# Two quarters of the last pair turned by TensorE, their input loaded early, and the last two products laced

## The chip, the cores and the metric

The kernel runs on one core of one Trainium2 chip. The metric is the device time of one execution in microseconds (us), the median over several runs; smaller is better. A profiled execution, taken by the hardware profiler, gives the trace from which the rows below come.

## The reference

One transformer-like block on `x` of 2 x 2048 x 512 in float32, with a condition vector per batch that gives six rows of shifts, scales and gates:

```python
emb = jnp.dot(jax.nn.silu(t), ada_w) + ada_b
shift_msa, scale_msa, gate_msa, shift_mlp, scale_mlp, gate_mlp = jnp.split(emb, 6, axis=-1)
norm = _ln(x) * (1.0 + scale_msa[:, None]) + shift_msa[:, None]
h = jax.nn.gelu(jnp.dot(norm, ssm_w1) + ssm_b1, approximate=False)
ssm_out = jnp.dot(h, ssm_w2) + ssm_b2
x = x + gate_msa[:, None] * ssm_out
norm2 = _ln(x) * (1.0 + scale_mlp[:, None]) + shift_mlp[:, None]
hf = jax.nn.gelu(jnp.dot(norm2, ff_w1) + ff_b1, approximate=True)
ff_out = jnp.dot(hf, ff_w2) + ff_b2
x = x + gate_mlp[:, None] * ff_out
```

`ff_w1` is 512 x 1024 and `ff_w2` 1024 x 512. The last two lines are the part that the change touches.

## The kernel before

The 4096 rows are cut into eight blocks of 512. The first half of the block (norm1, ssm1, ssm2, norm2) runs block by block; its result x1 goes to DRAM (`x1_d`). The feed-forward then takes the blocks in four pairs (`s` = 0 to 3): `up(s)` makes the hidden layer, `down(s)` the output. All products are made by Strassen's scheme in two levels: an outer product of a pair is cut into seven (P1 to P7), each of these again into seven *leaves* (P1 to P7), and a leaf is two matmuls of 128 x 128 by 256, four rows `128x256` in the trace.

**Order of TensorE's work.** `ff()` writes it out by hand in *slots*: the product number n starts at slot 7n, and its leaves stand two slots apart, in the order P1, P5, P6, P2, P7, P3, P4. So the second half of one product's leaves alternates with the first half of the next one's: the two are *laced*. `down` takes its products in the order P1, P2, P3, P6, P5, P7, P4. In the kernel before, the very last product (P4 of `down(3)`) starts six slots later (`starts[-1] += 6`) and is not laced: P7's leaves end first.

**Order of the other engines' work.** The class `Plan` collects every operation with its costs; `order()` gives each a latest time (`late`) by going back from the due times of TensorE's work, and `simulate()` plays the engines with these costs and picks, on each engine, the operation that is ready with the earliest latest time. Additions out of SBUF may go to VectorE or GpSimd (`"vg"`), whichever the simulation gives them to. The order that comes out is fixed for the chip. The outputs at the very end have no successor; for those that are named in `plan.closing` the due time is the end of TensorE's planned work plus 6000 ns.

**A quarter's way out.** The result of a pair stands transposed (features by rows) in `summed`, four quarters `r` = 0 to 3 of 128 x 2 x 512: r0 is finished by P2, r3 by P5, r2 by P7 and r1 by P4. r0 and r3 belong to the pair's first and second block in the first half of the columns and come from `quarter_out(s, 0, ...)`; r1 and r2 are the first and second block in the other half. To be added to x1 and stored, a quarter must be turned back. `quarter_out` (line 1065) does this in steps: two activations (bias and gate) by ScalarE, two transpositions of 32 x 32 blocks by VectorE into `bands` (`far` in the trace), four stores to DRAM (`back<-far`), one load back (`rows<-back`), the load of x1 into `rest` (`far<-x` or `near<-x`), two additions and two stores of the output. In the last pair the stores alternate between the queues of SP and ACT. For r1 and r2 of the last pair the gate is folded into the accumulation (`scaled_add`, line 1049), with the bias put in ahead by ScalarE.

In the kernel before, r1 of the last pair alone leaves by another way, `last_out`: as each of its four pieces (`quad`: half e of the columns, half h of the rows) is finished by a leaf, TensorE turns it in two transpositions of 128 x 128 (`turn_by_pe`, line 306) into a PSUM bank, VectorE adds it to x1, which was loaded into `near`, and the piece is stored, by SP's queue for e = 0 and by ACT's for e = 1. The turning of a piece stands one leaf behind the leaf that finished it.

The names of the trace: `rows` is `summed`, `hidden` the hidden layer of the pair, `near` and `far` hold operands, sums, `bands` and `rest`, and `back` is the DRAM copy. L258 is an addition (`tt`), L276 and L285 ScalarE's work, L296 a matmul, L306 a transposition by TensorE, L318 any DMA, L1049 `scaled_add`, L1073 a transposition by VectorE.

Of the kernel before, what the change touches and what calls it, by code (L numbers as in the profile page):

```python
# [20 lines left out]
class Plan:  # L21
# [67 lines left out]
    def order(self):  # L89
        ops = self.ops  # L90
        for op in ops:
            if op.engs == "p":
                op.deps = {d for d in op.deps if ops[d].engs != "p"}
            for d in op.deps:
                ops[d].succ.append(op.n)
        t, due = 0.0, {}
        for op in ops:
            if op.engs == "p":
                due[op.n] = t
                t += op.cost["p"]  # L100
        due.update((n, t + 6000.0) for n in self.closing)
        for _ in range(2):
            for op in reversed(ops):
                late = due.get(op.n, 1e9)
                for s in op.succ:
                    late = min(late, ops[s].late - (1 + op.care) * (self.HOP + min(op.lat.values()) + op.size / self.RATE))
                op.late = late - op.sooner
            self.simulate()
            wait = ops[self.anchor].start - due[self.anchor]
            due = {n: t + wait for n, t in due.items()}  # L110
        return sorted(ops, key=lambda op: (op.start, op.n))
# [89 lines left out]
def kernel(  # L201
# [21 lines left out]
    C = 4  # L223
# [836 lines left out]
    def rest_in(s, d, blk, x):  # L1060
        half = slice(d * D // 2, (d + 1) * D // 2)
        dma(x, x1_d[2 * s + blk][:, :, half])
        return x, out_blk[2 * s + blk][:, :, half]

    def quarter_out(s, d, blk, r, scaled=False):
        done = summed[:, r]
        n = quarters[0] % 2
        for e in range(0 if scaled else 2):
            act(done[:, e], done[:, e], AF.Identity, *columns(s, d, e, blk))
        band = cut(bands[n], "p (a c e r) -> p e c a r", a=M, c=C, e=2)  # L1070
        for e in range(2):
            o, a = band[:, e], cut(done[:, e], "p (c a q) -> p c a q", c=C, a=M)
            plan.add("v", lambda E, o=o, a=a: E.transpose(o, a), [o], [a], {"v": 636}, {"v": 705})  # L1073
        closing = s + 1 == NBLK // 2
        queue = lambda f: "sa"[f % 2] if closing else "s"
        far_t = back_d[s][d][blk]
        for f in range(M):
            dma(far_t[:, f].rearrange("(a q) r -> q a r", a=M), cut(bands[n][f * G : (f + 1) * G], "p (a r) -> p a r", a=M), queue(f))
        flat = done.rearrange("p e t -> p (e t)")
        dma(flat, far_t.rearrange("p f r -> p (f r)"))  # L1080
        x, to = rest_in(s, d, blk, rest[n])
        for h in range(2):
            c = slice(2 * h, 2 * h + 2)
            o = cut(x[:, c], "p c (e f r) -> p (c e) f r", e=2, f=M)
            a = cut(flat, "p (f c e r) -> p c e f r", f=M, c=C, e=2)[:, c].rearrange("p c e f r -> p (c e) f r")
            tt("v" if closing else "vg", o, a, o, ALU.add)
            if closing:
                dma(to[:, c], x[:, c], queue(h))
                plan.closing.append(plan.ops[-1].n)
        if not closing:  # L1090
            dma(to, x)
        quarters[0] += 1

    def down(s):
# [22 lines left out]
        def leaf(n, f):  # L1117
            p = DOWN[n]
            bank = chain_banks(14 * s + 7 + n)
            t = bank[BANK[f]][:, :HT]  # L1120
            for k in range(2):
                mm(t, fw2_leaves[p][f][:, k, :], inner[n][f][:, k, :], f in ("P1", "P5") and k == 0, f in ("P2", "P3", "P4") and k == 1)
            if f == "P1":
                copy(bank["x"][:, :HT], t)
                return
            quad = QUAD[f]
            e, h = int(quad[0]) - 1, int(quad[1]) - 1
            new = f not in ("P7", "P3")
            part = summed[:, :, e, h * HT : (h + 1) * HT]
            r0, r1, r2, r3 = [part[:, r] for r in range(4)]  # L1130

            def add(o, a):
                tt("v", o, t, a, ALU.add)

            if p in ("P1", "P3"):
                o = r1 if p == "P1" else r3
                if new:
                    copy(o, t)
                else:
                    add(o, o)  # L1140
            elif p == "P2":
                add(r0, r1 if new else r0)
                if f == "P4":
                    quarter_out(s, 0, 0, 0)
            elif p == "P6":
                add(r1, r1)
            elif p == "P5":
                add(r2, r1 if new else r2)
                if f in ("P2", "P7", "P3", "P4"):
                    tt("vg", r3, r3, r2, ALU.add)  # L1150
                    if last:
                        act(part[:, 1:3], part[:, 1:3], AF.Identity, *columns(s, 1, e, 0))
                if f == "P4":
                    quarter_out(s, 0, 1, 3)
            elif p == "P7":
                both, wide = part[:, 1:3], t.unsqueeze(1).to_broadcast([P, 2, HT])
                if last:
                    scaled_add(both, wide, columns(s, 1, e, 0)[1])
                else:
                    tt("v", both, wide, both, ALU.add)  # L1160
                if f == "P4":
                    quarter_out(s, 1, 1, 2, last)
            elif not last:
                add(r1, r1)
                if f == "P4":
                    quarter_out(s, 1, 0, 1)
            else:
                scaled_add(r1, t, columns(s, 1, e, 0)[1])
                last_out(s, f, quad)

        return sums, last_sum, prepare, leaf

    tail = {}

    def last_out(s, f, quad):
        if not tail:
            tail["x"], tail["out"] = rest_in(s, 1, 0, cut(kb(near_r, 0, 4), "p (c d) -> p c d", c=C))

        def turned_back(quad):
            e, h = int(quad[0]) - 1, int(quad[1]) - 1  # L1180
            bank = cut(banks[(2, 0)[h]], "p (c e d) -> p c e d", c=2, e=2)
            for c in range(2):
                col = slice((2 * h + c) * P, (2 * h + c + 1) * P)
                turn_by_pe(bank[:, c, e], summed[:, 1, e, col], ident, c == 0 and h not in tail, c == 1)
            tail[h] = True
            c, d = slice(2 * h, 2 * h + 2), slice(e * P, (e + 1) * P)
            x = tail["x"][:, c, d]
            tt("v", x, bank[:, :, e], x, ALU.add)
            dma(tail["out"][:, c, d], x, "sa"[e])

        tail.setdefault("due", [])
        for q in tail["due"]:
            turned_back(q)
        tail["due"] = []
        if f in ("P7", "P2", "P3", "P4"):
            tail["due"].append(quad)
        if f == "P4":
            turned_back(quad)

    def ff():  # L1200
        work, hooks = [], {}

        def at_slot(n, fn):
            hooks.setdefault(n, []).append(fn)

        for s in range(NBLK // 2):
            first_at = 14 * s
            got = {}

            def begin(s=s, got=got):  # L1210
                got["up"] = up(s, tokens(s))

            at_slot(7 * first_at, begin)
            for n in range(7):
                work.append((f"ff1 {s}", lambda n=n, got=got: got["up"][0](n), lambda f, n=n, got=got: got["up"][1](n, f)))
            sums, last_sum, prepare, leaf = down(s)
            at_slot(7 * (first_at + 7) + 7, sums)
            at_slot(7 * (first_at + 7 + 4) + 3, last_sum)
            for n in range(7):
                work.append((f"ff2 {s}", lambda n=n, fn=prepare: fn(n), lambda f, n=n, fn=leaf: fn(n, f)))  # L1220
        total = len(work)
        starts = [7 * n for n in range(total)]
        starts[-1] += 6
        for at in range(starts[-1] + 13):
            for fn in hooks.get(at, ()):
                fn()
            for n in range(max(0, at // 7 - 2), min(total, at // 7 + 1)):
                stage, prepare, leaf = work[n]
                plan.stage = stage
                if at == starts[n]:  # L1230
                    prepare()
                j, odd = divmod(at - starts[n], 2)
                if not odd and 0 <= j < 7:
                    leaf(CARRIED[j])

    def small_loads():
# [204 lines left out]
```

## Time and profile before

| | |
|---|---|
| median of 3 runs | 570.07 us (569.95 to 570.16) |
| the profiled execution's own time | 569.9 us |
| its span, first to last instruction | 568.1 us |
| mean granted clock of TensorE | 0.992 |
| busy: TensorE, VectorE, ScalarE, GpSimd | 553.2, 481.9, 281.6, 391.5 us |
| moved by DMA | 124.73 MB, mean 220 GB/s |

The span is shorter than the execution's time, since the latter has the start and the end around it. Busy times are sums over the whole span, and say little of its end, where the engines fall idle one after another; there the rows of the timeline say when each step began and how long it took.

### The profile page before, as it was taken

What the parts mean: (1) busy time and instruction counts of PE and PEld (TensorE: products, weight loads), DVE (VectorE), ACT (ScalarE), POOL (GpSimd) and SP (SyncE); (2) the same over time, 40 slices, a digit from 0 to 9 for tenths busy, and PEclk for the clock granted to TensorE, in tenths of its full rate; (3) what the DMA queues carried; (4) which work ended last, traced back from release to release, by engine and by line L of the source; (5) the groups of instructions that cost most, each with busy time, mean ns of one, the idle gap of its engine ahead of it and who ended that gap; (6) DMA issues with size and microseconds to landing.
All of it is one profiled execution on the core that took longest, in us unless ns stands there. A gap on an engine that the chain in (4) does not pass through costs nothing. (4 is left out here: it accounts for less than half of the span.)

```text
span 568.1 us, 8720 instructions
## 1 busy us (share of the span) xinstructions
PE 553.2 (97%) x2801; PEld 480.6 (85%) x2801; DVE 481.9 (85%) x841; ACT 281.6 (50%) x521; POOL 391.5 (69%) x476
## 2 busy tenths in 40 slices
PE   8999999999999999999999999999999999999982
PEld 4888889888898988888878888888888888888871
DVE  5696888987878588999999986799987999988993
ACT  3464867574978844665214347224447124353230
POOL 2887747979936399984756776775867777756750
PEclk9999999999999999999999999999999999999996
DMA  8953899988399969993203998404998405963238
GB/s 313 399 217 87 240 355 292 340 260 275 96 285 326 321 245 270 329 299 114 74 2 98 302 336 310 149 1 130 310 342 277 136 0 157 335 205 111 75 101 269
DMA packets 66209, 124.73 MB, mean 220 GB/s; under 512 B 5700, under 2 KB 33268, under 8 KB 64628
## 3 DMA queue, kind: packets, MB, share of 16 engines
q1 hardware_dynamic: 63856, 122.32, 65.3%
q10 hardware_dynamic: 2308, 1.86, 1.2%
q8 instruction: 22, 0.36, 0.3%
q14 instruction: 23, 0.19, 0.1%
HBM read 78.41 MB, written 44.70 MB: 217 GB/s over the span
## 5 line engine op out<-in xcount | busy, mean ns | idle before, releaser
L296 PE MATMUL bank<-turned,ring 128*128 128x256 f32 x896 | 210.2, 380 | 0.2 <-DVE turned L660 0.2
L296 PEld LDWEIGHTS bank<-turned,ring 128*128 128x128 f32 x896 | 167.9, 190 | 23.2 <-DVE turned L660 0.4
L258 DVE TENSOR_TENSOR hidden<-bank,hidden 128x512 f32<-128x512 f32 (+1 forms) x170 | 123.1, 753 | 23.2 <-PE bank L296 19.8
L296 PE MATMUL bank<-near,hidden 128*128 128x256 f32 (+1 forms) x470 | 95.1, 350 | 0.0
L296 PEld LDWEIGHTS bank<-near,hidden 128*128 128x128 f32 x470 | 82.2, 190 | 9.4 <-POOL near L258 0.3
L258 POOL TENSOR_TENSOR turned<-turned 128x512 f32<-128x512 f32 (+1 forms) x65 | 73.6, 1146 | 22.1 <-DVE turned L258 10.2
L296 PE MATMUL bank<-far,fw 128*128 128x256 f32 (+1 forms) x354 | 86.1, 375 | 0.2
L296 PE MATMUL bank<-ring 128*128 128x256 f32 x336 | 82.7, 380 | 0.1
L258 DVE TENSOR_TENSOR rows<-bank,rows 128x256 f32<-128x256 f32 (+1 forms) x142 | 65.9, 477 | 15.4 <-PE bank L296 12.6
L285 ACT COPY bank<-bank 128x512 f32<-128x512 f32 (+2 forms) x84 | 37.7, 449 | 75.2 <-PE bank L296 68.9
L296 PEld LDWEIGHTS bank<-far,fw 128*128 128x128 f32 x354 | 66.5, 190 | 10.0 <-issue 0.5
L296 PEld LDWEIGHTS bank<-ring 128*128 128x128 f32 x336 | 63.5, 190 | 9.8 <-issue 0.5
L276 ACT ACTIVATE hidden<-hidden,cols 128x512 f32<-128x512 f32 (+1 forms) x66 | 44.4, 709 | 42.1 <-DVE hidden L258 42.0
L258 POOL TENSOR_TENSOR hidden<-hidden 128x128 f32<-128x128 f32 (+2 forms) x45 | 45.7, 1025 | 26.7 <-DVE hidden L258 13.2
L296 PE MATMUL bank<-near,fw 128*128 128x256 f32 (+1 forms) x246 | 60.9, 377 | 0.4 <-DVE rows L1049 0.4
L296 PE MATMUL bank<-hidden,fw 128*128 128x256 f32 (+1 forms) x216 | 53.2, 376 | 1.1 <-DVE rows L1049 1.1
L296 PEld LDWEIGHTS bank<-near,fw 128*128 128x128 f32 x246 | 46.3, 190 | 6.9 <-issue 0.8
L276 ACT ACTIVATE turned<-turned,mod,mod 128x512 f32<-128x512 f32 x56 | 42.3, 806 | 9.3 <-DMA turned<-turned 8.9
L296 PEld LDWEIGHTS bank<-hidden,fw 128*128 128x128 f32 x216 | 40.3, 190 | 7.3 <-DVE rows L1049 1.5
L258 POOL TENSOR_TENSOR fw<-fw 128x256 f32<-128x256 f32 (+1 forms) x38 | 35.6, 945 | 12.0 <-DMA fw_parts<-fw 4.4
L258 POOL TENSOR_TENSOR ring<-turned,ring 128x256 f32<-128x256 f32 x41 | 29.8, 738 | 16.8 <-PE bank L296 9.2
L276 ACT ACTIVATE rows<-rows,gb,mod 128x512 f32<-128x512 f32 x32 | 25.5, 812 | 27.0 <-DVE rows L258 18.9
(124 smaller groups left out, 740.5 us busy)
## 6 DMA issues: line engine op xcount, KB each, us to landing
ring<-fw_parts SPq DMA_DIRECT2D x28, 512.0 KB, 4.3
turned<-far SPq DMA_DIRECT2D x52, 256.0 KB, 4.6
ring<-fw_parts SPq DMA_DIRECT2D x28, 384.0 KB, 5.5
turned<-turned SPq DMA_DIRECT2D x32, 256.0 KB, 4.9
rows<-back SPq DMA_DIRECT2D x15, 512.0 KB, 5.7
back<-far SPq DMA_DIRECT2D x54, 128.0 KB, 3.1
fw_parts<-fw SPq DMA_DIRECT2D x21, 256.0 KB, 4.6
fw<-in_L_cond_ada_w_dram SPq DMA_DIRECT2D x5, 1024.0 KB
```

What stands on the lines that cost most here:

```text
L258: lambda E: E.tensor_tensor(o, a, b, f),
L276: lambda E: E.activation(o, a, func, bias=bias, scale=scale),
L285: plan.add("a", lambda E: E.copy(o, a), [o], [a], {"a": cost}, {"a": cost + 60})
L296: lambda E: E.matmul(o, lhsT, rhs, start=start, stop=stop, skip_group_check=True, **kw),
```

## The change

- r2 of the last pair leaves the way r1 does: `last_out` becomes `turned_by_pe(blk, r, ...)`, which serves both. r1 (`blk` 0) is turned into banks 3 and 4, r2 (`blk` 1) into banks 2 and 0. r0 and r3 still go by `quarter_out`.
- The turning of a piece stands two leaves behind the leaf that finished it, counted over P7 and P4 together (their leaves other than P1); what is left after the last leaf is turned then.
- x1 for r1 and r2 is loaded into `hidden`, into the room of an operand of P1 (before: `near` for r1, `far` for r2).
- P4 starts at slot 7n like every other product and is laced with P7. Its operand sums are prepared six slots earlier with it.
- The outputs of r1 and r2 are named in `plan.closing`, and the due time of the closing outputs is the end of TensorE's work plus 3000 ns.

```diff
-        due.update((n, t + 6000.0) for n in self.closing)
+        due.update((n, t + 3000.0) for n in self.closing)
...
-    def quarter_out(s, d, blk, r, scaled=False):
+    def quarter_out(s, d, blk, r):
         done = summed[:, r]
         n = quarters[0] % 2
-        for e in range(0 if scaled else 2):
+        for e in range(2):
             act(done[:, e], done[:, e], AF.Identity, *columns(s, d, e, blk))
...
-                if f == "P4":
-                    quarter_out(s, 1, 1, 2, last)
+                if last:
+                    turned_by_pe(1, 2, f, quad)
+                elif f == "P4":
+                    quarter_out(s, 1, 1, 2)
...
                 scaled_add(r1, t, columns(s, 1, e, 0)[1])
-                last_out(s, f, quad)
+                turned_by_pe(0, 1, f, quad)
...
-    tail = {}
-
-    def last_out(s, f, quad):
-        if not tail:
-            tail["x"], tail["out"] = rest_in(s, 1, 0, cut(kb(near_r, 0, 4), "p (c d) -> p c d", c=C))
-
-        def turned_back(quad):
+    TURNED_AT = ((3, 4), (2, 0))
+    tail, waiting, leaves_read = [{}, {}], [], [0]
+
+    def turned_by_pe(blk, r, f, quad):
+        got = tail[blk]
+        if not got:
+            got["x"], got["out"] = rest_in(NBLK // 2 - 1, 1, blk, cut(kb(hidden_r, 8 * blk, 4), "p (c d) -> p c d", c=C))
+
+        def turned_back():
             e, h = int(quad[0]) - 1, int(quad[1]) - 1
-            bank = cut(banks[(2, 0)[h]], "p (c e d) -> p c e d", c=2, e=2)
+            bank = cut(banks[TURNED_AT[blk][h]], "p (c e d) -> p c e d", c=2, e=2)
             for c in range(2):
                 col = slice((2 * h + c) * P, (2 * h + c + 1) * P)
-                turn_by_pe(bank[:, c, e], summed[:, 1, e, col], ident, c == 0 and h not in tail, c == 1)
-            tail[h] = True
+                turn_by_pe(bank[:, c, e], summed[:, r, e, col], ident, c == 0 and h not in got, c == 1)
+            got[h] = True
             c, d = slice(2 * h, 2 * h + 2), slice(e * P, (e + 1) * P)
-            x = tail["x"][:, c, d]
+            x = got["x"][:, c, d]
             tt("v", x, bank[:, :, e], x, ALU.add)
-            dma(tail["out"][:, c, d], x, "sa"[e])
-
-        tail.setdefault("due", [])
-        for q in tail["due"]:
-            turned_back(q)
-        tail["due"] = []
+            dma(got["out"][:, c, d], x, "sa"[e])
+            plan.closing.append(plan.ops[-1].n)
+
+        n = leaves_read[0] = leaves_read[0] + 1
         if f in ("P7", "P2", "P3", "P4"):
-            tail["due"].append(quad)
-        if f == "P4":
-            turned_back(quad)
+            waiting.append((n, turned_back))
+        done = blk == 0 and f == "P4"
+        while waiting and (done or waiting[0][0] + 2 <= n):
+            waiting.pop(0)[1]()
...
-        starts = [7 * n for n in range(total)]
-        starts[-1] += 6
-        for at in range(starts[-1] + 13):
+        for at in range(7 * (total - 1) + 13):
...
-            for n in range(max(0, at // 7 - 2), min(total, at // 7 + 1)):
+            for n in range(max(0, at // 7 - 1), min(total, at // 7 + 1)):
                 stage, prepare, leaf = work[n]
                 plan.stage = stage
-                if at == starts[n]:
+                if at == 7 * n:
                     prepare()
-                j, odd = divmod(at - starts[n], 2)
-                if not odd and 0 <= j < 7:
+                j, odd = divmod(at - 7 * n, 2)
+                if not odd and j < 7:
                     leaf(CARRIED[j])
```

## The prediction

> **What bounds the kernel now.** I read the page first: it says which engine carries the span as a whole.
>
> ```profile
> span 568.1 us, 8720 instructions
> PE 553.2 (97%) x2801; PEld 480.6 (85%) x2801; DVE 481.9 (85%) x841; ACT 281.6 (50%) x521; POOL 391.5 (69%) x476
> ```
>
> TensorE is busy for 97% of the span, so only the stretches in which it is not can give time back. The view by windows shows where they are (columns: PE, PEld, DVE, ACT and POOL busy, clock, DMA share, GB/s).
>
> ```profile
> 520.00:530.00 10.00, 10.00 (x48) 8.79 (x47) 9.29 (x12) 3.64 (x8) 6.80 (x6) 1.00 0.00 0
> 545.00:550.00 5.00, 3.92 (x18) 3.10 (x18) 4.90 (x9) 3.13 (x5) 5.00 (x5) 1.00 0.00 0
> 550.00:553.00 3.00, 2.71 (x13) 2.05 (x11) 3.00 (x7) 0.36 (x1) 0.27 (x1) 1.00 0.84 203
> 553.00:557.00 4.00, 3.53 (x19) 2.75 (x19) 2.96 (x9) 0.00 (x0) 0.00 (x0) 1.00 1.04 275
> 557.00:568.00 11.00, 0.43 (x2) 0.20 (x2) 3.28 (x6) 0.00 (x0) 0.00 (x0) 0.62 0.81 274
> ```
>
> Three things are to be seen. Up to 545 us TensorE has no gap (the row of 520 to 530 stands for the ones before). From 545 to 553 VectorE is full (7.90 of 8 us) and TensorE is short of 1.4 us: VectorE sets the pace. After 557 both are done and 11 us pass with the DMA engines at 0.81. The change touches only the last two stretches, so I next took the end of the chain of waits (start, us, what), and the transfers of the last quarters by the timeline of SP and ACT.
>
> ```profile
> 557.47 0.43 DVE near L258
> 557.93 5.46 DMA out_dram<-near
> 563.38 0.68 DVE far L258
> ...
> 529.58 0.80 SPq L318 DMA_DIRECT2D back<-far  x2
> 533.36 0.34 SPq L318 DMA_DIRECT2D rows<-back  x1
> 549.57 0.78 SPq L318 DMA_DIRECT2D back<-far  x2
> 552.66 1.45 SPq L318 DMA_DIRECT2D back<-far  x2
> 554.29 0.76 SPq L318 DMA_DIRECT2D rows<-back  x1
> 555.36 0.82 SPq L318 DMA_DIRECT2D far<-x  x1
> 557.37 0.34 SPq L318 DMA_DIRECT2D rows<-back  x1
> 560.88 1.45 SPq L318 DMA_DIRECT2D out_dram<-near  x3
> 564.70 0.38 ACTq L318 DMA_DIRECT2D out_dram<-far  x1
> ```
>
> The chain names a DMA to out_dram as what released the add at 563.38, but an add can't wait for an output of another tile. What it reads is rows, and the rows<-back load issued at 557.37 is r2's: so that load is the true releaser, 6.0 us after its issue. VectorE's rows show both DRAM trips.
>
> ```profile
> 547.37 1.56 DVE L1049 SCALAR_TENSOR_TENSOR rows<-bank,mod,rows 128x512 f32<-128x512 f32 x2
> 548.84 0.70 DVE L1073 STREAM_TRANSPOSE far<-rows 128x512 f32<-128x512 f32 x1
> 550.10 1.32 DVE L258 TENSOR_TENSOR far<-rows,far 128x512 f32<-128x512 f32 x2
> 551.35 1.29 DVE L1073 STREAM_TRANSPOSE far<-rows 128x512 f32<-128x512 f32 x2
> 557.47 0.42 DVE L258 TENSOR_TENSOR near<-bank,near 128x256 f32<-128x256 f32 x1 [0.20 <-PE bank L306]
> 560.16 1.29 DVE L258 TENSOR_TENSOR near<-rows,near 128x512 f32<-128x512 f32 x2 [2.27 <-DMA rows<-back]
> 563.38 1.29 DVE L258 TENSOR_TENSOR far<-rows,far 128x512 f32<-128x512 f32 x2 [1.92 <-DMA out_dram<-near]
> ```
>
> r3 (product P5): second transposition at 548.84, stores from 549.57, load at 554.29, back at 560.16. r2 (product P7): transpositions at 551.35, stores from 552.66, load at 557.37, back at 563.38. From there the two adds, the output issued at 564.70 and its landing take 568.1 - 563.38 = 4.7 us. r1 (product P4), which TensorE turns already, has its last add at 557.47 and ends well before. So the end is set by r2's trip, and 3.2 us before it stands r3's.
>
> **The change part by part.** *r2 leaves the DRAM path.* Gone are two transpositions (1.29 us of VectorE), four stores and one load of 0.5 MB each way, one x1 load in the crowded stretch (555.36) and the two late adds. With r2 gone r3 is late next. If r3's trip stayed as it is, the end would be 560.16 + 4.7 = 564.9, a gain of 3.2 us.
>
> *What r2 costs instead.* Eight transpositions by TensorE and four adds out of PSUM. Their prices stand in the trace for r1:
>
> ```profile
> 544.03 1.03 PE L296 MATMUL bank<-hidden,fw 128*128 128x256 f32 x4
> 546.14 1.99 PE L296 MATMUL bank<-hidden,fw 128*128 128x256 f32 x8 [1.08 <-DVE rows L1049]
> 553.15 1.10 PE L296 MATMUL bank<-near,fw 128*128 128x256 f32 x4 [0.43 <-DVE rows L1049]
> 554.09 0.38 PE L306 MATMUL bank<-far,rows 128*128 128x128 f32 x2
> 554.30 1.03 PE L296 MATMUL bank<-near,fw 128*128 128x256 f32 x4
> 555.17 0.38 PE L306 MATMUL bank<-far,rows 128*128 128x128 f32 x2
> 555.39 1.03 PE L296 MATMUL bank<-far,fw 128*128 128x256 f32 x4
> 556.25 0.42 PE L306 MATMUL bank<-far,rows 128*128 128x128 f32 x2
> ```
>
> A pair of transpositions delays the next matmul by 554.30 - 554.09 = 0.21 us, so r2's four pairs cost TensorE 0.84 us; a leaf takes 0.86 us (555.39 to 556.25). The four adds are 0.42 each, 1.7 us of VectorE, 0.4 more than the transpositions they replace. All of it lies ahead of r1's last add, none of it ahead of r3's load except one or two adds.
>
> *P7 and P4 laced.* After P7's fourth leaf at 544.03 ten leaves are left: 10 x 0.86 = 8.6 us, with r2's 0.84 and one pair of r1's 0.21, which puts the end of the last leaf at 544.03 + 0.86 + 9.7 = 554.6 if nothing stalls, against 556.25 now. VectorE will not allow all of that: it is full from 545 to 553, and its work up to P4's last add only grows by the 0.4 while an add of r1 (0.42) falls behind it. So the end of the products comes earlier by at most what VectorE idles there now, about 1.1 us (553 to 557: 4 - 2.96). I take 0.7: r1's last add ends at 557.2 and its output is out, by the 3.4 us that the output at 564.70 needed, at 560.6, or, by the 5.5 of the chain's row, at 562.7. Either is ahead of r3. If the cover fails, r1 may grow by 1 us before it matters.
>
> *r3's trip gets quieter.* It took 549.57 to 560.16, 10.6 us. The same trip of r0 ran with the DMA engines to itself: stores at 529.58, load at 533.36, last bytes in the slice before 537.0:
>
> ```profile
> 536.50:537.00 0.50, 0.50 (x4) 0.45 (x3) 0.50 (x1) 0.00 (x0) 0.50 (x1) 1.00 0.06 25
> ```
>
> that is 7.4 us. Between these lies the after: during r3's trip r2's 0.5 MB store and the 0.5 MB x1 load fall away and r2's 0.5 MB of output comes in their place, 0.5 MB less, which at 275 GB/s (553 to 557) is 1.9 us. I take 10.6 - 1.9 = 8.7 us. The Trainium skill, DMA: Bandwidth & Descriptors, section "Issuing engines are not separate DMA queues", says that transfers issued from SP and from ACT run on the same 16 engines and interleave; by that rule r2's outputs on ACT's queue hold up r3's trip on SP's, and if they did not, the trip would be the quiet 7.4 and the end 1.3 us sooner. The trace agrees with the rule: a DMA share of 1.04 from 553 to 557, while both queues were at work. The two x1 loads cost nothing: their room is free once P1 is through, and the DMA engines are idle (0.00) from 520 to 530; were they to come after 550 instead, they would add 1.9 us each.
>
> *r3's start.* P4's sums are prepared six steps earlier, so some may fall to VectorE, ahead of r3's transpositions. The nearest rows are P7's sums, which are laced already: VectorE did three of the four, the planner's choice.
>
> ```profile
> 536.33 1.22 DVE L258 TENSOR_TENSOR hidden<-hidden 128x512 f32<-128x512 f32 x1
> 538.67 1.93 DVE L258 TENSOR_TENSOR far<-hidden,far 128x512 f32<-128x512 f32 x1
> 544.61 1.27 POOL L258 TENSOR_TENSOR far<-near 128x512 f32<-128x512 f32 x1 [1.58 <-DVE rows L258]
> L258 DVE TENSOR_TENSOR rows<-rows x3: 410/424/2016, 541.3 to 544.0; 128x256 f32<-128x256 f32 x3
> ```
>
> Now GpSimd does P4's (the row at 544.61 is the first), is free for them from there, and VectorE is the fuller one, so I expect half a sum or so on VectorE, 0.7 us. The bounds: a gain of 0.8 (the closings' due time is 3 us nearer, so the second transposition may pass the 0.78 us scaled add ahead of it) to a loss of 1.9 (one sum at its dearest). The Trainium skill, SBUF — State Buffer, section "Who interferes with whom", speaks against this part: a VectorE instruction with two SBUF inputs is blocked whole while GpSimd reads SBUF. The trace agrees: r3's own sums, rows<-rows, take 410 ns and once 2016. By the rule one of r3's sums could wait out a GpSimd sum of 1.27 us, which is within these bounds.
>
> **The sum.** r3's stores 549.57 + 0.7 = 550.3; back at + 8.7 = 559.0; end at + 4.7 = 563.7, a gain of 4.4 us. The profiled execution took 569.9 us for a span of 568.1, and the median of the runs is 570.07, so 2.0 lies around the span: 565.7 us. Its own range: at best 549.57 - 0.8 + 7.4 + 4.7 = 560.9, 562.9 us; at worst 549.57 + 1.9 + 10.6 + 4.7 = 566.8, 568.8 us. That bytes alone do not bind: from 549.57 on there are r3's store, load and output and the outputs of r0, r1 and r2, 6 x 0.5 MB, at 275 GB/s 11.4 us, which ends at 561.
>
> **The rivals.** *A: r3's load is stuck on SP's queue.* SP issues in the written order, and r1's and r2's outputs now have due times too. An output of r1 on SP waits for TensorE and VectorE; if the planner puts r1's last SP output ahead of r3's load, the load goes at 556.6 to 557.4 instead of 554. Back after 3.6 us (r0's, 533.36 to 537.0) to 6.0 us (r2's), the end is 564.9 to 568.1: 566.9 to 570.1 us. For it: the planner counts a store trip longer than it took (549.57 to 554.29). Against: the load is due ahead of the outputs by its own trip and the adds behind it, so it is taken as soon as the planner holds it to be ready. Chance 0.15.
>
> *B, the slower side: P4's four sums go to VectorE.* Place: VectorE between 543 and 553, where it has 0.1 us to spare. Price: four times 1.2 to 1.9 us, 4.9 to 7.7 us on every add behind them. r1's last add would end at 557.9 + 4.9 to 7.7, and with 3.4 to 5.5 us for its output the span is 566.2 to 571.1; sums of 1.6 us and the output that the chain shows give 557.9 + 6.4 + 5.5 = 569.8, 571.8 us. It is slower from 5.8 us of sums on (557.9 + 5.8 + 5.5 = 569.2, 1.1 above the span now). For: VectorE took three of P7's four. Against: GpSimd is busy only 0.27 us from 550 to 553 and nothing else is planned for it. Chance 0.10.
>
> *C: the trip does not shorten.* r2's outputs and r0's, planned earlier, fill the engines as r2's trip did, and r3's stores come 1.9 us later on top: the upper end of the forecast, 568.8, up to 570. Chance 0.05.
>
> **How the numbers follow.** Forecast 0.70, A 0.15, B 0.10, C 0.05. The predicted time is the forecast's, 565.7. About 0.2% is what a measurement here can tell from no change, 1.1 us: faster means below 568.9. The forecast lies below it, and two thirds of A, one fifth of B, half of C: 0.70 + 0.10 + 0.02 + 0.02 = 0.84, of which I take 0.02 off for the forecast's upper edge: 0.82. Same takes the rest of A and C and that edge, 0.08; slower is most of B and what I can't see, 0.10. The range goes from the forecast's lower end, 562.9, to 569.2, which takes in its upper end and most of A and leaves out B: about 0.15.
>
> **What would show it.** Right: two rows<-back loads after 520 us instead of three; no transposition after r3's; r3's load before 555 and back before 560; the last adds of the span on the near tile, the last output 3 to 4 us before the end; two x1 loads into hidden before 540. TensorE's last instruction at about 556.7. Wrong: r3's load after 556 (A), P4's sums far<-near among VectorE's rows after 543 (B), a trip of more than 10 us from stores to adds (C), or a gap of TensorE before 540, which would mean that the order changed upstream.

## The result, and the profile after

The change takes 565.65 us (median of 4 runs, 565.55 to 565.75) against 570.12 us of the kernel before in the same comparison: a ratio of 0.9921, with a 95% interval of 0.9904 to 0.9938, 4.5 us less. The profiled execution took 565.75 us with a span of 564.0.

The windows of the kernel after, at the end of its span (columns as before: PE, PEld, DVE, ACT and POOL busy, clock, DMA share, GB/s):

```profile
545.00:550.00 5.00, 4.86 (x25) 3.95 (x24) 4.90 (x9) 2.89 (x5) 2.55 (x2) 1.00 0.00 0
550.00:553.00 3.00, 3.00 (x16) 2.37 (x16) 3.00 (x7) 0.00 (x0) 0.00 (x0) 1.00 0.70 165
553.00:557.00 4.00, 3.03 (x19) 2.42 (x17) 3.80 (x11) 0.00 (x0) 0.00 (x0) 1.00 0.84 192
557.00:564.00 7.00, 0.17 (x2) 0.00 (x0) 2.04 (x4) 0.00 (x0) 0.00 (x0) 0.80 0.82 270
```

TensorE's gap of 1.4 us between 545 and 553 is nearly gone (7.86 of 8 us), VectorE is as full as it was, now up to 557, and the stretch after 557 has shrunk from 11 us to 7. The timeline of the kernel after, SP and ACT (DMA issues) and then VectorE and TensorE, shows what stands in it:

```profile
549.99 0.78 SPq L318 DMA_DIRECT2D back<-far  x2
551.68 0.40 SPq L318 DMA_DIRECT2D out_dram<-hidden  x1
553.72 0.40 SPq L318 DMA_DIRECT2D out_dram<-far  x1
554.35 0.34 SPq L318 DMA_DIRECT2D rows<-back  x1
560.15 0.38 ACTq L318 DMA_DIRECT2D out_dram<-near  x1
...
540.87 1.21 DVE L258 TENSOR_TENSOR near<-hidden,near 128x1024 f32<-128x1024 f32 x1
543.73 1.22 DVE L258 TENSOR_TENSOR far<-near,far 128x512 f32<-128x512 f32 x1
548.67 1.29 DVE L1073 STREAM_TRANSPOSE far<-rows 128x512 f32<-128x512 f32 x2
556.99 0.76 DVE L258 TENSOR_TENSOR hidden<-bank,hidden 128x256 f32<-128x256 f32 x2 [0.20 <-PE bank L306]
558.83 1.29 DVE L258 TENSOR_TENSOR near<-rows,near 128x512 f32<-128x512 f32 x2 [1.08 <-DMA rows<-back]
...
555.17 0.38 PE L306 MATMUL bank<-far,rows 128*128 128x128 f32 x2
556.52 0.66 PE L306 MATMUL bank<-far,rows 128*128 128x128 f32 x4 [0.97 <-DVE hidden L258]
```

One load from DRAM is left here, r3's. r1 and r2 are added into `hidden` and the last of these adds ends at 557.75. VectorE then has nothing to do until r3 is back at 558.83. The end of the chain of waits says it too:

```profile
553.09 0.60 DVE far L258
554.35 4.38 DMA rows<-back
558.83 0.69 DVE near L258
559.52 0.60 DVEq L1437
```

The chain doesn't reach the load by way of r3's stores. It comes from r0's first addition (553.09), whose output stands ahead of the load on SP's queue (553.72).

| step | forecast | measured |
|---|---|---|
| r3's stores | 550.3 | 549.99 |
| r3's load | 554 | 554.35 |
| r3 back, adds begin | 559.0 | 558.83 |
| from there to the end | 4.7 | 5.2 |
| span | 563.7 | 564.0 |
| r1's last add ends | 557.2 | 557.75 |

### The profile page after: what moved, and what is told of

The parts are those of the page before. It is cut to its first block, busy times and chain, and to the rows that moved or that the text cites. A ratio compares the mean times of both kernels' runs of the same rounds, so it can differ in the third digit from the quotient of the medians.

```text
span 564.0 us, 8729 instructions
## 1 busy us (share of the span) xinstructions
PE 552.8 (98%) x2809; PEld 481.2 (85%) x2809; DVE 481.4 (85%) x842; ACT 281.7 (50%) x521; POOL 388.5 (69%) x475
## 4 chain that ended last, share of the span: by engine, by line
PE 87%; DVE 7%; DMA 3%; ACT 1%; issue 1%; POOL 1%; DVEq 0%; SPq 0%; ACTq 0%
PE bank L296 87%; DVE rows L258 2%; DMA fw<-in_L_cond_ada_w_dram 1%; DVE near L258 1%; DVE rows L1049 1%; DVE fw L258 1%; DMA rows<-back 1%; DVE far L258 1%; DVE far L1073 1%; ACT rows L276 1%; DVE hidden L258 0%; DMA fw<-in_L_cond_ada_b_dram 0%; PE bank L306 0%; POOL hidden L258 0%; POOL near L258 0%
## 5 line engine op out<-in xcount | busy, mean ns | idle before, releaser
L258 DVE TENSOR_TENSOR hidden<-bank,hidden 128x512 f32<-128x512 f32 (+2 forms) x178 | 126.2, 738 | 23.8 <-PE bank L296 20.3
L258 POOL TENSOR_TENSOR hidden<-hidden 128x128 f32<-128x128 f32 (+2 forms) x46 | 46.9, 1029 | 28.4 <-DVE hidden L258 13.3
```

The costliest lines, as they stand in the source:

```text
L258: lambda E: E.tensor_tensor(o, a, b, f),
```

## The experiments

The medians below stand beside 570.15 to 570.26 us for the kernel before, run beside each group.

**1. The change without lacing** (`e1_unlaced`).

```diff
-        for at in range(7 * (total - 1) + 13):
+        starts = [7 * n for n in range(total)]
+        starts[-1] += 6
+        for at in range(starts[-1] + 13):
```

> The change with one part undone: P4 starts six slots later again, so P7 and P4 are not laced; r2 and r1 are still turned by TensorE. Theory T (the end is set by r3's DRAM trip; taking r2's trip away gave the gain, lacing only moves r1, which is not last): r3's stores start within 1 us of 549.99, its adds within 1 us of 558.83, the time is 565.0 to 566.7 us. Rival L (lacing gave the gain, r2's trip was covered): 568.5 to 570 us.

564.78 us (564.60 to 565.16; ratio to before 0.9907, 0.9892 to 0.9922). Rival L falls; and the kernel is 0.9 us faster than the change, just under the lower end of what theory T gave (r3's stores too moved by a little more than the 1 us that it allowed). Its timeline, SP and VectorE:

```profile
548.85 0.78 SPq L318 DMA_DIRECT2D back<-far  x2
553.26 0.80 SPq L318 DMA_DIRECT2D rows<-back  x1
548.12 0.70 DVE L1073 STREAM_TRANSPOSE far<-rows 128x512 f32<-128x512 f32 x1
557.70 0.76 DVE L258 TENSOR_TENSOR hidden<-bank,hidden 128x256 f32<-128x256 f32 x2 [0.53 <-PE bank L306]
558.37 1.28 DVE L258 TENSOR_TENSOR near<-rows,near 128x512 f32<-128x512 f32 x2
```

r3's stores go 1.14 us earlier than in the change, and r1's last add ends 0.7 us later (558.46). Lacing buys r1 0.7 us and costs r3 1.1, and r3 is the one that is last. Here r3's adds begin with no idle time before them, right behind r1's: the two ends have met.

**2. Lacing alone, on the kernel before** (`e2_laced_only`).

```diff
-        starts = [7 * n for n in range(total)]
-        starts[-1] += 6
-        for at in range(starts[-1] + 13):
+        for at in range(7 * (total - 1) + 13):
```

> The kernel before with one part of the change alone: P4 laced with P7, everything else as before (r2 through DRAM, closings due after 6000 ns). Theory T: r2's trip still ends last, and P7's last leaf comes three leaves of P4 later (2.6 us, of which VectorE's full stretch hides some), so r2's adds come at 564 to 566 in place of 563.4: 570.5 to 573 us, slower than before. Rival L: TensorE's stall of 1.1 us goes and everything behind it comes earlier: 566 to 569 us.

570.82 us (570.10 to 571.76; 1.0010, 1.0002 to 1.0019): slower by 0.1%, as theory T had it, at the low end of its range. In the profiled execution, the shortest of the eleven, r2's adds come at 563.62 in place of 563.38, where theory T had put them at 564 to 566. The way there was another one than expected, as SP's timeline shows:

```profile
555.88 0.40 SPq L318 DMA_DIRECT2D out_dram<-near  x1
557.53 0.56 SPq L318 DMA_DIRECT2D rows<-back  x1
```

An output of r1 now stands ahead of r3's and r2's loads on SP's queue, and it was late because TensorE had waited 2.52 us for VectorE (last section). r2's load, the one of 557.53, goes 0.16 us later than in the kernel before. This is the mechanism of the prediction's rival A.

**3. Closings due after 6000 ns again** (`e3_due_6000`).

```diff
-        due.update((n, t + 3000.0) for n in self.closing)
+        due.update((n, t + 6000.0) for n in self.closing)
```

> The change with the closing outputs due 6000 ns after TensorE's planned end again, in place of 3000. On VectorE one addition of r3 (rows<-rows) moves; SP's order is the same. Theory T: r3's stores move with that addition and nothing else does: within 0.7 us of the change, 565.2 to 566.4 us. Rival D (the nearer due time is what put r3's trip early): stores 2 us later or more, 567.5 to 569 us.

565.67 us (565.33 to 566.15): the change's time to 0.02 us. r3's stores came at 549.40, even a little earlier than in the change, since the addition that moved went to GpSimd. The due time is worth nothing that shows here; rival D falls.

**4. r0's additions on GpSimd** (`e4_r0_by_gpsimd`).

```diff
-            tt("v" if closing else "vg", o, a, o, ALU.add)
+            tt(("g" if r == 0 else "v") if closing else "vg", o, a, o, ALU.add)
```

> The change with one thing added: r0's two closing additions are given to GpSimd, which is idle from 548, so r0's output (0.5 MB) no longer stands between r3's stores and its load, and VectorE loses 1.3 us of work. Theory T with r3's trip lengthened by the bytes beside it: the trip falls from 8.84 us (stores to adds) to between 7.4 and 8.0, the time to 564.2 to 565.1 us. Rival (the trip is bound by its own latency, bytes beside it don't matter): 565.4 to 565.9 us.

565.58 us (565.23 to 567.26): no gain; the rival's number. (The profiled execution is the one of 567.26; it was 1.8 us late already at 545, so only differences within it are used.) SP's timeline shows where the freed bytes went:

```profile
551.09 0.40 SPq L318 DMA_DIRECT2D out_dram<-far  x1
551.82 0.80 SPq L318 DMA_DIRECT2D back<-far  x2
553.51 1.77 SPq L318 DMA_DIRECT2D out_dram<-hidden  x2
556.53 0.34 SPq L318 DMA_DIRECT2D rows<-back  x1
```

r0's output now goes right ahead of r3's stores in place of right behind them. From stores to load it is 4.71 us (4.36 in the change), and the adds begin 9.14 us after the stores (8.84). The output was moved from one half of the trip into the other. So the time of this run doesn't tell a trip bound by bytes from one bound by latency. Its trace says a little more: a store of r3 landed 4.2 us after its issue here, with r0's output beside it, and 3.3 us after it in the change. A fixed latency alone does not give that.

**5. r3 turned by TensorE too** (`e5_r3_by_pe`).

```diff
-                if f == "P4":
+                if last and f in ("P2", "P7", "P3", "P4"):
+                    act(r3, r3, AF.Identity, *columns(s, 0, e, 1))
+                    turned_by_pe(1, 3, f, quad)
+                elif f == "P4":
                     quarter_out(s, 0, 1, 3)
...
-    TURNED_AT = ((3, 4), (2, 0))
+    TURNED_AT = {1: (2, 0), 2: (3, 4), 3: (2, 0)}
```

> The change, and r3 is turned by TensorE too, piece by piece, so its trip through DRAM is gone; bias and gate of r3 are put in piece by piece by ScalarE; r3 uses the banks 2 and 0, r2 the banks 3 and 4, r1 then 2 and 0. Theory T (r3's trip sets the end of the change; next late is r1): r1's last add within 0.7 us of its 557.75 in the change, its output out 3.4 to 5.5 us later, the span 561.2 to 563.2, the time 562.9 to 564.9 us. Rival B (VectorE sets the end in any case, r3's trip was beside it): 565.2 to 566.5 us.

564.45 us (563.96 to 564.98; 0.9895, 0.9882 to 0.9909), 1.2 us less than the change and inside theory T's range; rival B falls. TensorE's and VectorE's timeline:

```profile
546.58 1.10 PE L296 MATMUL bank<-hidden,fw 128*128 128x256 f32 x4 [0.71 <-DVE rows L1049]
557.84 0.66 PE L306 MATMUL bank<-far,rows 128*128 128x128 f32 x4 [0.69 <-DVE hidden L258]
558.32 0.76 DVE L258 TENSOR_TENSOR hidden<-bank,hidden 128x256 f32<-128x256 f32 x2 [0.53 <-PE bank L306]
```

r1's last add now is the last work, at 559.08, and the span ends 3.1 us after it at 562.2. The add is 1.3 us later than in the change, where theory T allowed 0.7, and the output after it is quicker than the 3.4 to 5.5 us that it put, so the time fell into its range with two terms off. r3's trip was what the change ended with, and r1 stood little more than 1 us behind it.

**6. The same with r0's additions on GpSimd** (`e6_r3_pe_r0_gpsimd`; the edit of 4 on top of 5).

> As the kernel with r3 turned by TensorE, and r0's two additions on GpSimd, so VectorE has 1.3 us less to do between P7's and P4's last leaves. Theory T with r1 now last and VectorE its pace: 0.5 to 1.3 us less than with r0 on VectorE, 562.0 to 563.8 us. Rival (TensorE's own work is the pace there): no difference to it within 0.3 us.

564.63 us (564.34 to 564.83): no difference. VectorE has idle time between its adds there (2.98 of 4 us busy from 553 to 557, against 3.59 in 5), while TensorE is busy for all 4 us in both. So theory T's second half, that VectorE sets r1's pace, fell, and the rival held.

**7. r3 by TensorE, not laced** (`e7_r3_pe_unlaced`; the edit of 1 on top of 5).

> As the kernel with r3 turned by TensorE, but P4 starts six slots later, not laced. With r3's trip gone the end hangs on r1, so lacing should be worth something here where it cost 0.9 us in the change: 0.5 to 1.2 us more than the laced one. Rival (lacing costs wherever VectorE is full): 0.5 to 1 us less than the laced one.

565.19 us (565.10 to 565.39): 0.74 us more than the laced one by the medians, as theory T had it; the nearest two runs of the two kernels are 0.1 us apart. r1's last add ends at 560.23, 1.15 us later than laced. The same edit is worth 0.9 us in one direction in experiment 1 and 0.7 us in the other here; what differs is which quarter is last.

**8. x1 in the rooms of before** (`e8_x1_in_old_rooms`).

```diff
-            got["x"], got["out"] = rest_in(NBLK // 2 - 1, 1, blk, cut(kb(hidden_r, 8 * blk, 4), "p (c d) -> p c d", c=C))
+            got["x"], got["out"] = rest_in(NBLK // 2 - 1, 1, blk, rest[0] if blk else cut(kb(near_r, 0, 4), "p (c d) -> p c d", c=C))
```

> The change with x1 of r1 and r2 loaded where the kernel before had them, r1's into near, r2's into the room that r0 leaves. The loads come later, r2's only after r0's output; the planner answers by putting r0's additions ahead of P7's. Theory T (the room as such costs nothing as long as the loads come before 550): 564.8 to 566.3 us. Rival (a late x1 load of 0.5 MB stands in r3's trip): 1.9 us on top, 567 to 568 us.

566.70 us (566.54 to 567.38): 1.05 us more than the change, between the two. VectorE's and SP's timeline:

```profile
541.73 3.33 DVE L258 TENSOR_TENSOR far<-rows,far 128x512 f32<-128x512 f32 x2
559.70 0.76 DVE L258 TENSOR_TENSOR near<-bank,near 128x256 f32<-128x256 f32 x2 [0.53 <-PE bank L306]
560.38 1.28 DVE L258 TENSOR_TENSOR near<-rows,near 128x512 f32<-128x512 f32 x2
547.51 0.53 SPq L318 DMA_DIRECT2D far<-x  x1
551.01 0.79 SPq L318 DMA_DIRECT2D back<-far  x2
```

The load itself comes at 547.51, in a quiet stretch, and is not what costs. To make room for it r0's two adds stand ahead of r3's work, 3.33 us where they took 1.32 in the kernel before. r3's stores come 1.02 us later than in the change, but they are not what ends the span: TensorE waits for VectorE twice (1.59 us before 547.75, 1.25 us before 553.99), r1's last add ends at 560.46, 2.7 us later than in the change, and r3's adds follow right behind it without idle time. So r1's path is last here, and the missing room is paid for on it.

**9. P4's sums on GpSimd** (`e9_p4_sums_gpsimd`).

```diff
-            inner[n] = second(v, thirds(half_s[n % 2]), room=rooms[n % 3] if n < 4 else None)
+            inner[n] = second(v, thirds(half_s[n % 2]), "g" if last and n == 6 else "vg", room=rooms[n % 3] if n < 4 else None)
```

> The change with P4's four operand sums all given to GpSimd; in the change VectorE does one of them (far<-near,far at 543.73, 1.22 us) ahead of r3's transpositions. One addition of r3 goes to GpSimd with it. SP's order is the same. Theory T (lacing costs what it puts on VectorE ahead of r3's transpositions, and the end follows r3): r3's stores 1.0 to 1.8 us ahead of 549.99, the time 564.0 to 564.9 us. Rival (VectorE waits for P7's leaves there in any case): within 0.3 us of the change, 565.3 to 565.9.

564.89 us (564.82 to 565.20): 0.76 us less than the change, as theory T had it. r3's stores come at 548.91, 1.08 us earlier; its adds begin at 558.26, 0.57 earlier. This is nearly what lacing had cost in experiment 1, with the lacing kept. Half of what the stores gained was lost on the way. SP's timeline and a window:

```profile
552.97 0.40 SPq L318 DMA_DIRECT2D out_dram<-far  x1
553.59 0.39 SPq L318 DMA_DIRECT2D rows<-back  x1
553.00:554.00 1.00, 1.00 (x7) 0.87 (x6) 1.00 (x3) 0.00 (x0) 0.00 (x0) 1.00 0.20 64
```

r3's load stands behind r0's output on SP, as in the change, and that output waits for r0's first addition on VectorE. So the load goes 4.68 us after the stores (4.36 in the change), while the DMA engines' share is 0.20: it waits for its turn, not for bytes.

**10. P4's sums on VectorE** (`e10_p4_sums_vector`; `"v"` in place of `"g"`).

> The opposite: P4's four sums all on VectorE, the case that rival B of the prediction priced at 4.9 to 7.7 us and a time of 568.2 to 573.1. The order puts three of them behind r3's transpositions and r3's load ahead of r0's output on SP. Theory T: r3's stores within 0.5 us of 549.99, VectorE 2 to 4 us later at P4's last add (560 to 562), r1's output last, 565.5 to 568 us. Rival B as it was priced: 568.2 us or more.

566.19 us (565.91 to 566.62; 0.9930, 0.9918 to 0.9943). That is within theory T's range, and 2 us below the lowest price of rival B. r1's last add ends at 559.25, earlier than the 560 to 562 that theory T put, and r3's adds, right behind it, are the last work. The four sums on VectorE, GpSimd's last work, and SP's row of the load:

```profile
543.54 1.76 DVE L258 TENSOR_TENSOR far<-near 128x512 f32<-128x512 f32 x1
549.59 0.65 DVE L258 TENSOR_TENSOR far<-near,far 128x512 f32<-128x512 f32 x1
551.15 0.68 DVE L258 TENSOR_TENSOR near<-near 128x512 f32<-128x512 f32 x1
553.53 0.68 DVE L258 TENSOR_TENSOR far<-near,far 128x512 f32<-128x512 f32 x1
543.28 1.47 POOL L258 TENSOR_TENSOR far<-hidden,far 128x512 f32<-128x512 f32 x1
545.77 0.73 POOL L258 TENSOR_TENSOR rows<-rows 128x256 f32<-128x256 f32 x1 [1.03 <-DVE rows L258]
549.70 0.78 SPq L318 DMA_DIRECT2D back<-far  x2
553.41 0.34 SPq L318 DMA_DIRECT2D rows<-back  x1
```

The first sum ran beside GpSimd's of 543.28 and took 1.76 us; the other three ran after GpSimd's last instruction and took 0.65 to 0.68. Together 3.8 us, not 4.9 to 7.7. r3's load stands ahead of r0's output here and goes 3.71 us after the stores, 0.65 us sooner than in the change.

**11. r1 in four banks** (`e11_r3_pe_four_banks`, on top of 5).

```diff
+    LAST_AT = {"11": 2, "22": 0, "12": 5, "21": 3}
...
-            bank = cut(banks[TURNED_AT[r][h]], "p (c e d) -> p c e d", c=2, e=2)
+            bank = cut(banks[LAST_AT[quad] if r == 1 else TURNED_AT[r][h]], "p (c e d) -> p c e d", c=2, e=2)
```

> As the kernel with r3 turned by TensorE, but r1's four pieces go to four banks (2, 0, 5, 3) in place of two. There TensorE waited 0.69 us for VectorE to read the bank's other piece before the last two turnings (557.84). Theory: r1's last add 0.4 to 0.7 us earlier, and the end with it, 563.7 to 564.1 us. Rival (VectorE's own row of adds is the pace, TensorE's wait is idle time): the same as with two banks, 564.3 to 564.7.

563.61 us (563.59 to 565.17; 0.9891, 0.9877 to 0.9904): 0.84 us less than experiment 5 by the medians. The runs of the two overlap and so do their intervals, and the profiled executions differ by 0.4 us, so the size is not settled; that the wait went is seen in the trace. TensorE's and VectorE's last rows:

```profile
556.88 1.18 PE L306 MATMUL bank<-far,rows 128*128 128x128 f32 x6
557.48 1.07 DVE L258 TENSOR_TENSOR hidden<-bank,hidden 128x256 f32<-128x256 f32 x3
```

The three last turnings run without a wait, and VectorE's last adds end at 558.55 in place of 559.08.

**12. All of it** (`e12_all`: 11 and the edit of 9).

> r3 turned by TensorE, r1 in four banks, and P4's sums on GpSimd. Both of P4's sums that VectorE does there (1.21 and 0.68 us) leave it. Theory T: TensorE's wait of 0.71 us at 546.58 shrinks and P4's last add comes 0.5 to 1.2 us earlier than with the four banks alone: 562.7 to 563.6 us. Rival (TensorE's row of leaves and turnings is the pace): within 0.3 us of the four banks alone.

563.55 us (563.46 to 564.23; 0.9887, 0.9872 to 0.9902): no different from 11, as the rival had it. VectorE's row where the freed time went:

```profile
545.74 2.92 DVE L1049 SCALAR_TENSOR_TENSOR rows<-bank,mod,rows 128x512 f32<-128x512 f32 x4 [1.10 <-ACT rows L276]
```

The sums leave VectorE, and it waits 1.10 us for ScalarE's activation on r1 and r2 in their place. So TensorE's wait before 546.63 stays at 0.74 us, and from there on the chain of waits runs over TensorE's leaves and turnings to r1's last adds. These two kernels are the fastest, 2.1 us below the change.

## Why the prediction was right, and where it was not

**What ends the span.** The step "with r2 gone r3 is late next" held. That the lacing and the due time did not make the gain is shown by experiments 1 to 3, and that r3's trip was then the last thing by the chain of waits and by 5.

**r3's start.** The term was 0.7 us, and 0.42 was measured (549.99 against 549.57); but the two parts of it were not what the prediction put. Without lacing the stores come at 548.85, 0.72 us earlier than before: the gain that was named only as a bound (0.8) was there. Lacing takes 1.14 us back, where 0.7 was put. The prediction also looked for the cost in P4's four sums alone. One of them is on VectorE in the kernel after (543.73); experiment 9 moves it, and one addition of r3 with it, and gets 1.08 us. VectorE's share of P4's operand itself (near<-hidden, 540.87) is a further such cost, which the prediction did not name; no run took it away.

**What lacing is worth.** "I take 0.7" was said of r1's last add. Against the unlaced change it is 0.7 (557.75 against 558.46), against the kernel before only 0.1 (557.89). For the end the prediction booked only the 0.7 us on r3's start, and it cost 0.9 us there (experiment 1).

**The trip.** 8.7 us forecast, 8.84 measured. From stores to load it fell from 4.72 to 4.36 us, from load to adds from 5.87 to 4.48. That the trip lies above the quiet 7.4 is shown; that the bytes beside it are the reason is argued only. Experiment 4 moved 0.5 MB within the trip, not out of it, and no run made the trip quiet. Part of the 8.84 is not bytes: the load stood behind r0's output on SP, whose issue ended at 554.12, and with the order reversed it went 0.65 us sooner (experiment 10). The prediction hung the load on r3's stores alone. In the change it hung on VectorE's addition of r0; in experiment 9 stores that came 1.08 us earlier moved the load by only 0.76.

**From adds to end.** 4.7 forecast, 5.2 measured. The prediction took it from a moment when r1's outputs were through; here they were issued up to 558 and ran into r3's. That fits, but was not tested apart.

**The sum.** 563.7 forecast, 564.0 measured. That it came so near is in part luck. In r3's start a gain of 0.72 us that the sum did not take stood against a cost 0.44 us larger than it took. The trip got part of its length from an order on SP's queue that the sum did not have, and the stretch behind the adds was 0.5 us longer.

**r1's path.** Its last add was put at 557.2 and came at 557.75. The term left out is TensorE's wait of 0.97 us (556.52): the kernel's plan treats a bank as one place, so a turning may not write into it while VectorE still has to read the other piece there. Four banks take such a wait away (0.69 us, experiment 11).

**The x1 loads.** They stand at 517.25, far from the end, and nothing there waits for them. The room was worth 1.05 us, by the planner's answer to its absence and not by the load (experiment 8).

**The rivals.** A was there in small: 0.65 us, with an output of r0 ahead of the load and not of r1. B's mechanism is real, its price was not: the dear rows of 1.2 to 1.9 us were taken beside a working GpSimd, and P4's sums on VectorE mostly ran beside an idle one. The Trainium skill, SBUF — State Buffer, section "Who interferes with whom", says that a VectorE instruction with two inputs in SBUF contends with a GpSimd instruction that reads SBUF, and experiment 10 agrees: 1.76 us beside GpSimd, 0.65 to 0.68 without it. The prediction used the rule for r3's sums and left it out for the price of B.

## What to carry to other kernels

Take the last two or three chains apart from the trace, each with its own end: what a reordering is worth changes its sign with which of them is last (lacing: 0.9 us lost, then 0.7 us won). An addition's price read from a row holds only for what ran beside it there. The transposition through DRAM took 8.8 to 10.6 us of waiting at the end of these kernels and was worth replacing even by work on full engines, until the next chain was last. A transfer whose data are ready can still stand behind one on the same queue whose data are not: look at what is issued ahead of it.

## What the runs showed of the hardware

The clock fell in the middle of experiment 2. TensorE's timeline and the windows:

```profile
553.70 1.26 PE L296 MATMUL bank<-near,fw 128*128 128x256 f32 x4 [2.52 <-DVE rows L1049]
555.18 1.92 PE L296 MATMUL bank<-near,fw 128*128 128x256 f32 x4
554.00:554.50 0.50, 0.50 (x4) 0.45 (x3) 0.00 (x0) 0.00 (x0) 0.00 (x0) 1.00 1.00 285
555.00:556.00 1.00, 1.00 (x4) 0.86 (x3) 0.85 (x2) 0.00 (x0) 0.00 (x0) 0.50 0.98 274
558.00:559.00 1.00, 0.87 (x5) 0.51 (x4) 0.31 (x1) 0.00 (x0) 0.00 (x0) 1.00 1.06 279
```

After a gap of 2.52 us the granted clock was still 1.00 until 554.5, then 0.50 for some 3 us although TensorE was at work again, and 1.00 from 558. A leaf took 1.92 us in the trace in place of 1.03. Gaps of 0.97 us (the change), 1.08 us (the kernel before) and 1.59 us (experiment 8) had no such consequence. That the gap is the cause is read from this one trace; no run varied its length.
